# A fourth second-level product in a two-level Strassen MoE layer, with its mixtures, row transposes and output gates placed anew

## The chip, the cores and the metric

The kernel runs on one core of one Trainium2 chip. A core has five engines that work side by side, each through its own instructions in order: TensorE (PE) multiplies matrices and writes to PSUM, VectorE (DVE) and ScalarE (ACT) do elementwise work, GpSimd (POOL) issues the indirect DMAs here, and SyncE (SP) issues the plain ones. The metric is the device time of one execution in microseconds.

## The reference, cut to what matters

The input x is 8 sequences of 1024 tokens with 512 features, fp32. An attention layer with sine and cosine features comes first, and it is not touched here. Then follows a mixture of experts:

```python
x = x + attention(layernorm(x))
x = x + moe(layernorm(x))

# moe: 8 experts, 2 per token, at most 160 tokens of a sequence per expert
probs = softmax(x @ Wr + br); topk_p, topk_e = top_k(probs, 2)
buf = scatter(x)                          # (8 experts, 1280 rows, 512)
h = relu(einsum("enc,ech->enh", buf, W1) + b1)   # 512 -> 2048
y = einsum("enh,ehc->enc", h, W2) + b2           # 2048 -> 512
out = sum over a token's experts of topk_p * y
```

Each expert therefore multiplies 1280 rows by a 512 x 2048 and by a 2048 x 512 matrix, all in fp32.

## The kernel before, in words

Attention and most of the routing take the first 1260 us. The experts follow in 16 chunks, two per expert: a **long** chunk of 768 rows (`nh` = 3 blocks of 128 rows in each of two halves) and a **short** one of 512 rows (`nh` = 2). The even chunks 0, 2, ..., 14 are long, the odd ones short. `experts()` runs a chunk's first layer (`layer1`, eight steps `q`), and then its second layer.

Both layers use Strassen's scheme in Winograd's form: the two operands are cut into 2 x 2 blocks, and seven products p1 to p7 of sums and differences ("mixtures") of blocks take the place of eight. VectorE makes the mixtures: `mix_w1` for the first layer's weights, one step ahead; `mix_w2` for W2, in eight parts, for the expert to come, during a long chunk's first layer (one part in each step from the third on, the rest behind the eighth step); `gather` for the rows (the four row sums at L1185 to L1188). The hidden tile `hid` holds seven row parts (h11, h12, g4, h22, g1, g2, g3), which `p4` completes (relus on ScalarE at L1278 to L1281, sums on VectorE at L1282 to L1285).

In the second layer, `layer2` handles one block in each half with plain products (L1340); chunk 0 uses it for its three blocks, and each later long chunk for its third block. All other blocks go two at a time through `layer2_quad` (seven long chunks from chunk 2 on, and eight short ones). There a plain product is 32 matmuls of 256 columns (L1473). Three of the seven products, p2, p3 and p4, are cut once more by the same scheme: `mix` makes eight mixtures of 128 x 512 on VectorE (L1422 to L1429), and `second_level` runs seven chains of eight matmuls of 128 columns (L1439, through `chain`). In such a run three PSUM banks u, v and z are reused: a chain that adds onto u must wait until ScalarE has copied u out. ScalarE makes five copies (L1450, L1453, L1455, L1459, L1464), VectorE three adds (L1457, L1461, L1462). The counts of matmuls in the profile are two for each in the code, since an fp32 matmul shows as two.

The mixtures need room (`places`): a short chunk takes the unused columns of `hid`, a long one the rows' tiles `xe` and `xe_s`, which the first layer has finished with.

Rows arrive by an indirect DMA on GpSimd's queue (`fetch`), go through DRAM (`put_row`, `quarters` on SP's queue) and are transposed on VectorE (L1175). `gather` yields after each transpose; the generator `aside` carries it, and the second layer calls `next(aside)` between its products. A finished output row block is biased on VectorE, scaled by the router's probability on ScalarE (`gate`, L1310), and added to the output in DRAM by an indirect accumulating DMA on GpSimd's queue (`send`, L1315), two blocks in each half, first rows y1 and second rows y2.

The order on PE, ACT, DVE and SP is the order of the Python program (`manual_schedule`). GpSimd's instructions are placed by a planner. Pools are released tile by tile.

Of the kernel before, what the change touches and what calls it, by code (L numbers as in the profile page):

```python
# [73 lines left out]
def preln_attn_moe_kernel(  # L74
# [105 lines left out]
    load_x(0)  # L180
    ident = const.tile([P, P], F32, name="ident")
    make_identity(nc, ident)
# [1145 lines left out]

    def layer2(i, block, hid, aside):

        e = chunks[i][0]
        ws = w2_tiles[e]
        cols = slice(block * P, (block + 1) * P)

        def bank():
            return pools["ps_p"].tile([P, 512], F32, name="ps_p")[:, :DC]

        def product(ps, part, weight, first, last):
            for k in range(NHQ):
                nc.tensor.matmul(  # L1340
                    ps, lhsT=hid[:, k, part, cols], rhs=ws[weight][:, k, :],
                    start=first and k == 0, stop=last and k == NHQ - 1, skip_group_check=True,
                )
            next(aside, None)

        gate, send = outputs(i, block)
        (y1, y11, y12), (y2, y21, y22) = new_y(), new_y()
        low, high = b2_tiles[e][:, :DC], b2_tiles[e][:, DC:]

        def side_product():  # L1350
            side = bank()
            product(side, 1, 1, True, True)
            TT(y11, y11, side, ALU.add)

        plain_first = i == 0 and block == 0
        top = bank()
        product(top, 0, 0, True, False)
        nc.scalar.copy(y11, top)
        if plain_first:
            side_product()  # L1360
        mid = bank()
        product(mid, 4, 3, True, False)
        nc.scalar.copy(y22, mid)
        product(top, 5, 4, False, False)
        nc.scalar.copy(y12, top)
        if not plain_first:
            side_product()
            product(top, 6, 5, False, False)
            TT(y22, y22, top, ALU.add)
        product(mid, 2, 2, False, True)  # L1370
        TT(y12, y12, mid, ALU.add)
        TT(y1, y1, b2_tiles[e], ALU.add)
        gate(0, y1)
        send(0, y1)
        if plain_first:
            product(top, 6, 5, False, False)
            TT(y22, y22, top, ALU.add)
        TT(y22, y22, high, ALU.add)
        gate(1, y22)
        product(top, 3, 6, False, True)  # L1380
        TT(y21, top, low, ALU.add)
        gate(1, y21)
        send(1, y2)

    def places(i, hid):
# [15 lines left out]

    SECOND = [(1, 1), (2, 2), (3, 6)]

    def layer2_quad(i, hid, aside, before_last):

        e = chunks[i][0]
        ws = w2_tiles[e]
        free = places(i, hid)
        low, high = b2_tiles[e][:, :DC], b2_tiles[e][:, DC:]
        two = range(2)  # L1410

        def split(t, part_of):
            return [[part_of(t[:, 4 * k : 4 * k + 4], c) for c in two] for k in two]

        def mix(n):
            part, weight = SECOND[n]
            a = split(hid, lambda t, c: t[:, :, part, c * P : (c + 1) * P])
            b = split(ws[weight], lambda t, c: t[:, :, c * P : (c + 1) * P])
            (a11, a21), (a12, a22) = a
            (b11, b12), (b21, b22) = b  # L1420
            t1, t2, t3, t4, s2, s3, s4 = free[:7]
            TT(t1, b12, b11, ALU.subtract)  # L1422
            TT(s3, a11, a21, ALU.subtract)
            TT(a21, a21, a22, ALU.add)
            TT(t2, b22, t1, ALU.subtract)
            TT(s2, a21, a11, ALU.subtract)
            TT(t3, b22, b12, ALU.subtract)
            TT(s4, a12, s2, ALU.subtract)
            TT(t4, b21, t2, ALU.subtract)  # L1429
            return (  # L1430
                (a11, b11), (a12, b21), (s4, b22), (a22, t4), (a21, t1), (s2, t2), (s3, t3)
            )

        def bank():
            return pools["ps_p"].tile([P, 512], F32, name="ps_p")

        def chain(ps, pair, first):
            for k in range(4):
                nc.tensor.matmul(  # L1439
                    ps, lhsT=pair[0][:, k, :], rhs=pair[1][:, k, :], start=first and k == 0,  # L1440
                    stop=k == 3, skip_group_check=True,
                )

        def second_level(n, pairs):
            m1, m2, m3, m4, m5, m6, m7 = pairs
            c = free[7 + n]
            c11, c12, c21, c22 = (c[:, k, :] for k in range(4))
            u, v, z = (bank()[:, :P] for _ in range(3))
            chain(u, m1, True)
            nc.scalar.copy(c11, u)  # L1450
            next(aside, None) if n < 2 else None
            chain(v, m5, True)
            nc.scalar.copy(c21, v)  # L1453
            chain(u, m6, False)
            nc.scalar.copy(c12, u)  # L1455
            chain(z, m2, True)
            TT(c11, c11, z, ALU.add)  # L1457
            chain(u, m7, False)
            nc.scalar.copy(c22, u)  # L1459
            chain(v, m3, False)  # L1460
            TT(c22, c22, c21, ALU.add)  # L1461
            TT(c12, c12, v, ALU.add)  # L1462
            chain(u, m4, False)
            nc.scalar.copy(c21, u)  # L1464
            return [c[:, 2 * b : 2 * b + 2, :] for b in two]

        def as_pair(t):
            return t.rearrange("p (c n) -> p c n", n=P)

        def product(ps, part, weight, first, last):  # L1470
            for b in two:
                for k in range(NHQ):
# [5 lines left out]
                    )  # L1478

        gate, send = zip(*(outputs(i, b) for b in two))  # L1480
        some(2, aside)
        pairs = mix(0)
        top, mid = bank(), bank()
        of = lambda ps, b: ps[:, b * DC : (b + 1) * DC]
        y1, y11, y12 = zip(*(new_y() for _ in two))
        product(top, 0, 0, True, False)
        for b in two:
            nc.scalar.copy(y11[b], of(top, b))
        next(aside, None)
        product(mid, 4, 3, True, True)  # L1490
        some(3, aside)
        c = second_level(0, pairs)
        for b in two:
            TT(as_pair(y11[b]), as_pair(y11[b]), c[b], ALU.add)
        pairs = mix(1)
        product(top, 5, 4, False, False)
        for b in two:
            nc.scalar.copy(y12[b], of(top, b))
            TT(y12[b], y12[b], of(mid, b), ALU.add)
        c = second_level(1, pairs)  # L1500
        for b in two:
            TT(as_pair(y12[b]), as_pair(y12[b]), c[b], ALU.add)
        y2, y21, y22 = zip(*(new_y() for _ in two))
        for b in two:
            nc.scalar.copy(y22[b], of(mid, b))
        for b in two:
            TT(y1[b], y1[b], b2_tiles[e], ALU.add)
            gate[b](0, y1[b])
            send[b](0, y1[b])
        pairs = mix(2)  # L1510
        product(top, 6, 5, False, True)
        for b in two:
            TT(y22[b], y22[b], of(top, b), ALU.add)
            TT(y21[b], of(top, b), low, ALU.add)
            TT(y22[b], y22[b], high, ALU.add)
        before_last()
        c = second_level(2, pairs)
        for b in two:
            TT(as_pair(y21[b]), as_pair(y21[b]), c[b], ALU.add)
            gate[b](1, y22[b])  # L1520
            gate[b](1, y21[b])
            send[b](1, y2[b])


# [18 lines left out]
    def experts(ending):  # L1543
# [5 lines left out]
        for i, (e, j0, nh) in enumerate(chunks):  # L1549
            parts, box = box[0], [None]  # L1550
            hid = pools["hp"].tile([P, NHQ, 7, HALF], F32, name="hid")
            tiles = None
            ahead = rows_ahead(i + 1) if i and i + 1 < len(chunks) else iter(())
            for q in range(NHQ):
# [5 lines left out]
                if i and q > 1:  # L1560
                    next(mixes, None)
                next(ahead, None)
                tiles = layer1(Hidden(i, q, parts, hid, [ending]), tiles, q == NHQ - 1)
                if i == 0 and q == NHQ // 2:
                    rest(ending)
                    to_router.close()
                    for name, bufs in (("w2p", 1), ("yp", 4), ("bp", 1)):
                        pools[name] = to_end.pool(name, bufs, reuse_waits="tile", **left)
# [19 lines left out]
            if i:  # L1588
                layer2_quad(
                    i, hid, iter(()) if nh > 2 else aside, mix_next if nh == 2 else lambda: None  # L1590
                )
            for block in range(2 if i else 0, nh):
                if block == nh - 1:
                    mix_next()
                layer2(i, block, hid, aside)
            rest(aside)
# [253 lines left out]
```

## Time and profile before

| | |
|---|---|
| median of 3 runs | 3204.99 us (3201.2 to 3208.88) |
| the profiled execution | 3195.52 us; span 3193.8 us |
| PE busy | 3122.6 us (98%) |
| DVE busy | 2209.3 us (69%) |
| ACT busy | 1664.9 us (52%) |
| POOL busy | 426.8 us (13%) |
| a plain product in a quad, 32 matmuls | 6.91 us |
| a second-level run, 56 matmuls | 6.25 us |
| a long chunk: first layer, quad, third block | 72.25, 46.38, 24.18 us |
| a short chunk: first layer, quad | 48.35, 46.38 us |

How to read it: busy shares are averages over stages with different limits, so a share far below 100% says nothing of a stage. The chain that ended last is followed back from the last instruction, each step to what released it. In the profile's timelines a row gives start, length, engine, line, operation, output and inputs, and in brackets the idle time before it with what ended that. TensorE's matmuls are pipelined, so consecutive ones overlap in the timeline; the spacing of their starts is what they cost. A row with a count (x8) merges several instructions.

### The profile page before, as it was taken

Reading aid. Unit: us, or ns where it says so; the run is one execution under the profiler, and the core shown is the slowest. Engines: PE = TensorE matmul, PEld = TensorE weight load, DVE = VectorE, ACT = ScalarE, POOL = GpSimd, SP = SyncE. Lnnn points to the kernel's source line nnn. Section 1 sums busy time; section 2 is a strip of 40 time slices with the busy share of each in tenths; the row PEclk is TensorE's granted clock in tenths of the full one; section 3 lists DMA queues with packets and bytes.
Section 4 is the critical chain, followed back from the end, with each engine's and each line's share of the span. In section 5 each row is a group of like instructions: output and inputs, shape, how many; then the busy total and the mean of one; then the engine's idle time right before and its main releaser. Section 6 shows DMA issues by size and latency. Waiting matters only on the chain.

```text
span 3193.8 us, 51293 instructions
## 1 busy us (share of the span) xinstructions
PE 3122.6 (98%) x19726; PEld 2145.4 (67%) x19726; DVE 2209.3 (69%) x4643; ACT 1664.9 (52%) x2554; POOL 426.8 (13%) x387
## 2 busy tenths in 40 slices
PE   5999999999999999999999999999999999999998
PEld 2444444444444444689698698698698698698687
DVE  8888878888788775637657657656657656656654
ACT  7888888888888885413423423323323323323322
POOL 3000202020111123411011011011011011011010
PEclk9999999999999999999999999999999999999999
DMA  5435454554645353423423433434433334334331
GB/s 166 147 100 165 120 159 132 148 140 138 184 108 159 80 166 88 141 60 98 147 57 98 140 62 103 130 63 112 120 70 110 115 74 114 107 80 116 96 60 21
DMA packets 288547, 358.72 MB, mean 112 GB/s; under 512 B 28376, under 2 KB 199088, under 8 KB 276272
## 3 DMA queue, kind: packets, MB, share of 16 engines
q1 hardware_dynamic: 264944, 312.20, 33.3%
q0 software_dynamic: 22912, 43.22, 7.4%
q8 instruction: 157, 2.57, 0.4%
q14 instruction: 86, 0.70, 0.1%
q10 hardware_dynamic: 448, 0.02, 0.0%
HBM read 207.02 MB, written 81.22 MB: 90 GB/s over the span
## 4 chain that ended last, share of the span: by engine, by line
PE 79%; DVE 3%; ACT 1%; issue 1%; DMA 0%; SPq 0%; POOLq 0%; DVEq 0%; ACTq 0%
PE ps_p L1239 30%; PE ps_p L1473 13%; PE av L717 9%; PE ps_p L1439 9%; PE ps_s L683 9%; PE ps_p L1340 7%; ACT e L703 1%; PE ps_s L215 1%; PE ps_s L697 1%; DVE qk_f L524 1%; DVE qk_r L447 0%; DVE xT L837 0%; DMA qk<-qk_r 0%; DVE v L447 0%; SPq L608 0%
## 5 line engine op out<-in xcount | busy, mean ns | idle before, releaser
L703 ACT ACTIVATE e<-ps_s 128x1024 f32<-128x1024 f32 (+1 forms) x640 | 569.6, 937 | 183.3 <-PE ps_s L683 110.2
L683 PE MATMUL ps_s<-qk 64*128 64x512 f32 (+3 forms) x3072 | 597.3, 505 | 28.6 <-DMA qk<-qk_r 12.4
L717 PE MATMUL av<-e,v 128*64 128x512 f32 (+3 forms) x3072 | 523.4, 490 | 0.0
L683 PEld LDWEIGHTS ps_s<-qk 64*128 64x128 f32 x3072 | 262.3, 187 | 216.1 <-issue 106.4
L717 PEld LDWEIGHTS av<-e,v 128*64 128x64 f32 x3072 | 200.5, 137 | 283.1 <-issue 267.1
L1239 PE MATMUL ps_p<-xe,w 128*128 128x256 f32 (+1 forms) x1024 | 317.6, 433 | 1.1 <-issue 1.1
L1239 PE MATMUL ps_p<-xe_s,t 128*128 128x256 f32 (+1 forms) x1024 | 317.7, 433 | 0.0
L1239 PE MATMUL ps_p<-xe,t 128*128 128x256 f32 (+1 forms) x1024 | 317.7, 433 | 0.0
L1315 POOL DMA_INDIRECT out_dram<-y,slots x80 | 127.1, 1589 | 1234.0 <-ACT y L1310 1016.6
L768 POOL DMA_INDIRECT slot_d<-token,slot x128 | 159.2, 1244 | 988.5 <-issue 612.3
L1282 DVE TENSOR_TENSOR hid<-hid 128x256 f32<-128x256 f32 (+1 forms) x128 | 64.0, 500 | 283.0 <-ACT hid L1280 283.0
L1239 PEld LDWEIGHTS ps_p<-xe_s,t 128*128 128x128 f32 x1024 | 193.8, 190 | 82.0 <-ACT hid L1249 2.5
L1239 PEld LDWEIGHTS ps_p<-xe,t 128*128 128x128 f32 x1024 | 194.2, 190 | 80.4 <-issue 0.4
L1239 PEld LDWEIGHTS ps_p<-xe,w 128*128 128x128 f32 x1024 | 193.7, 190 | 79.4 <-issue 1.2
L1473 PE MATMUL ps_p<-w_t,hid 128*128 128x256 f32 x960 | 212.2, 379 | 0.0
L1473 PE MATMUL ps_p<-w,hid 128*128 128x256 f32 x960 | 209.6, 379 | 0.0
L1473 PEld LDWEIGHTS ps_p<-w,hid 128*128 128x128 f32 x960 | 182.4, 190 | 26.3
L1473 PEld LDWEIGHTS ps_p<-w_t,hid 128*128 128x128 f32 x960 | 180.1, 190 | 23.2
L1239 PE MATMUL ps_p<-xe_s,w 128*128 128x256 f32 (+1 forms) x512 | 158.9, 433 | 0.6 <-ACT p L1255 0.6
L1249 ACT COPY hid<-ps_p 128x256 f32<-128x256 f32 (+1 forms) x128 | 54.2, 423 | 179.6 <-PE ps_p L1239 170.9
L1340 PE MATMUL ps_p<-w,hid 128*128 128x256 f32 x640 | 144.8, 381 | 2.5 <-DVE w L1068 2.5
L697 PEld LDWEIGHTS <-keys_b 64*128 64x128 bf16 x1536 | 80.8, 95 | 89.5 <-issue 71.5
(300 smaller groups left out, 4959.6 us busy)
## 6 DMA issues: line engine op xcount, KB each, us to landing
w<-in_L_ffn_W_dram SPq DMA_DIRECT2D x256, 256.0 KB, 3.4
w<-in_L_ffn_W_dram SPq DMA_DIRECT2D x64, 512.0 KB, 7.4
qk<-qk_c SPq DMA_DIRECT2D x124, 256.0 KB, 4.5
qk<-qk_r SPq DMA_DIRECT2D x120, 256.0 KB, 4.5
qk_base<-base_d SPq DMA_DIRECT2D x28, 1024.0 KB, 7.5
xn_d<-xn SPq DMA_DIRECT2D x72, 256.0 KB, 2.4
rows_d<-xg SPq DMA_DIRECT2D x70, 256.0 KB, 2.1
x_mid<-in_L_attn_x_dram SPq DMA_DIRECT2D x16, 1024.0 KB, 8.9
```

The lines of the kernel that those rows point to most:

```text
L683: nc.tensor.matmul(ps[:, a, at : at + w], lhsT=pair[r, 1, kb * P : (kb + 1) * P], rhs=pair[r, 0, q0 : q0 + w], start=at == 0, stop=not own ...
L697: nc.tensor.matmul(out_, lhsT=keys_b[r, part, :], rhs=late, start=False, stop=part == 1, skip_group_check=True,)
L703: nc.scalar.activation(e, ps[:, :, :n], AF.Exp, scale=UNIT * UNIT / math.sqrt(2 * DH))
L717: nc.tensor.matmul(av[a * 64 : (a + 1) * 64, q0 - 512 * h :], lhsT=vt[:, kb, 2 * pr + a, :], rhs=es[i][:, a, at : at + w], start=kb == 0, ...
L768: queued = nc.gpsimd.indirect_dma_start(out=slot_d[b], out_offset=bass.IndirectOffsetOnAxis(ap=idx, axis=0), in_=src, in_offset=None,)
L1239: nc.tensor.matmul(ps, lhsT=weights[:, k, :], rhs=rows[:, k, :], start=first and k == 0, stop=last and k == 1, skip_group_check=True,)
L1249: nc.scalar.copy(self.blocks[0], self.top)
L1282: TT(g1, g3, h22, ALU.add)
L1315: ins = nc.gpsimd.indirect_dma_start(out=out, out_offset=bass.IndirectOffsetOnAxis(ap=meta[:, e, jj[r], 0:1], axis=0), in_=y, in_offset=No ...
L1340: nc.tensor.matmul(ps, lhsT=hid[:, k, part, cols], rhs=ws[weight][:, k, :], start=first and k == 0, stop=last and k == NHQ - 1, skip_group ...
L1439: nc.tensor.matmul(ps, lhsT=pair[0][:, k, :], rhs=pair[1][:, k, :], start=first and k == 0, stop=k == 3, skip_group_check=True,)
L1473: nc.tensor.matmul(ps[:, b * DC : (b + 1) * DC], lhsT=hid[:, k, part, b * P : (b + 1) * P], rhs=ws[weight][:, k, :], start=first and k == ...
```

## The change

The quad's fourth product, p5, is cut by the second level too. Its plain product, 32 matmuls of 256 columns, becomes a run of seven chains, 56 matmuls of 128 columns, and the bank `mid` that held it is gone; the result goes from a tile c5 into y12 and y22. The second level is now a class `Second` with `weights`, `left` (the eight mixtures), `both` (all eight in an interleaved order) and `run` (the seven chains), where `run` takes two callbacks: `between`, behind the first copy, and `late`, behind the fourth. In short chunks the weight mixtures of p5 and p2 are made during the first layer (`early_sums`), two in each of the steps 4 to 7; in long chunks p5's eight are made at the quad's start. The order of products in a quad is now p1, p5, p6, p2, p7, p3, p4; in long chunks two products of the third block stand ahead of p4, the others behind the quad.

W2's parts for the next expert are made one in each of the third and fourth steps of the long first layer, and two in each step from the fifth. The row transposes of a short chunk come two ahead of p5's run, one behind the next eight mixtures, one inside p2's run, one behind p4's mixtures, and the last one with the four row sums inside p3's run; in long chunks they come in two pairs among the third block's products. The gates of the right halves go behind the first copy of p4's run, and in short chunks the gates and sends of the first rows go behind its fourth copy. There are five y buffers in place of four, and the identity matrix moves to a pool that ends with the routing. `layer2` is a generator.

```diff
-    ident = const.tile([P, P], F32, name="ident")
+    ident = own.tile([P, P], F32, name="ident")
...
-    SECOND = [(1, 1), (2, 2), (3, 6)]
+    class Second:
+        OPERANDS = {2: (1, 1), 3: (2, 2), 4: (3, 6), 5: (4, 3)}
...
+        def weights(self):
...
+            for to, x1, x2 in ((t3, b22, b12), (t1, b12, b11), (t2, b22, t1), (t4, b21, t2)):
+                TT(to, x1, x2, ALU.subtract)
+                yield
+
+        def left(self):
...
+            for to, x1, x2, op in (
+                (s3, a11, a21, ALU.subtract), (a21, a21, a22, ALU.add),
+                (s2, a21, a11, ALU.subtract), (s4, a12, s2, ALU.subtract),
+            ):
+                TT(to, x1, x2, op)
+                yield
+
+        def both(self):
+            w, a = self.weights(), self.left()
+            for gen, count in ((w, 2), (a, 2), (w, 1), (a, 1), (w, 1), (a, 1)):
+                some(count, gen)
...
+        def run(self, c, between=lambda: None, late=lambda: None):
...
+            chain(u, a11, b11, True)
+            nc.scalar.copy(c11, u)
+            between()
+            chain(v, a21, t1, True)
+            nc.scalar.copy(c21, v)
+            chain(u, s2, t2, False)
+            nc.scalar.copy(c12, u)
+            chain(z, a12, b21, True)
+            TT(c11, c11, z, ALU.add)
+            chain(u, s3, t3, False)
+            nc.scalar.copy(c22, u)
+            late()
+            chain(v, s4, b22, False)
+            TT(c22, c22, c21, ALU.add)
+            TT(c12, c12, v, ALU.add)
+            chain(u, a22, t4, False)
+            nc.scalar.copy(c21, u)
...
-        some(2, aside)
-        pairs = mix(0)
-        top, mid = bank(), bank()
+        ask(2)
+        if last_part:
+            rest(second[5].left())
+        else:
+            rest(second[5].weights())
+            rest(second[5].left())
+        top = bank()
...
-        product(mid, 4, 3, True, True)
-        some(3, aside)
-        c = second_level(0, pairs)
+        if last_part:
+            rest(second[2].left())
+        ask(2)
+        five = second[5].run(c5)
+        second[3 if last_part else 2].both()
+        ask()
         product(top, 5, 4, False, False)
...
+        add_to(y12, five)
+        add_to(y11, second[2].run(c, ask))
+        second[4 if last_part else 3].both()
+        ask()
+        product(top, 6, 5, False, True)
...
+        add_to(y12, second[3].run(c, ask))
         for b in two:
             TT(y1[b], y1[b], b2_tiles[e], ALU.add)
...
+        if not last_part:
+            first_rows()
+            second[4].both()
+            some(2, extra)
+        before_last()
...
+        add_to(y21, second[4].run(c5, right_halves, first_rows if last_part else lambda: None))
         for b in two:
-            gate[b](1, y22[b])
             gate[b](1, y21[b])
             send[b](1, y2[b])
...
-                    next(mixes, None)
+                    some(1 if q < 4 else 2, mixes)
...
+                if 2 < q < 7:
+                    some(2, early_sums)
...
-                    for name, bufs in (("w2p", 1), ("yp", 4), ("bp", 1)):
+                    for name, bufs in (("w2p", 1), ("yp", 5), ("bp", 1)):
...
+                if nh > 2:
+                    some(2, aside)
+                    for step in range(5):
+                        if step == 4:
+                            mix_next()
+                        next(extra)
+                        if step < 2:
+                            some(2, aside)
```

Here `ask` advances `aside` in short chunks alone, `some(n, g)` takes n steps of a generator and `rest(g)` all that are left; `extra` is the third block's `layer2`; `right_halves` and `first_rows` are the gates, with the sends, named above; `before_last` makes the next chunk's first W1 mixtures in short chunks.

More of the change, by code (lines that the diff above doesn't have):

```diff
@@ L1 @@
+import itertools
 import math
@@ L1327, in new_y, with layer2 @@
         return y, y[:, :DC], y[:, DC:]
-    def layer2(i, block, hid, aside):
+    def layer2(i, block, hid):
         e = chunks[i][0]
@@ L1343, in product @@
                 )
-            next(aside, None)
         gate, send = outputs(i, block)
-        (y1, y11, y12), (y2, y21, y22) = new_y(), new_y()
+        y1, y11, y12 = new_y()
         low, high = b2_tiles[e][:, :DC], b2_tiles[e][:, DC:]
[L1350 to L1353, printed above, removed]
         plain_first = i == 0 and block == 0
@@ L1358, in layer2 @@
         nc.scalar.copy(y11, top)
+        yield
         if plain_first:
-            side_product()
+            side = bank()
+            product(side, 1, 1, True, True)
+            TT(y11, y11, side, ALU.add)
+            yield
         mid = bank()
         product(mid, 4, 3, True, False)
+        yield
+        y2, y21, y22 = new_y()
         nc.scalar.copy(y22, mid)
@@ L1365, in layer2 @@
         nc.scalar.copy(y12, top)
+        yield
         if not plain_first:
-            side_product()
+            side = bank()
+            product(side, 1, 1, True, True)
+            TT(y11, y11, side, ALU.add)
+            yield
             product(top, 6, 5, False, False)
             TT(y22, y22, top, ALU.add)
+            yield
         product(mid, 2, 2, False, True)
@@ L1374, in layer2 @@
         send(0, y1)
+        yield
         if plain_first:
@@ L1377, in layer2 @@
             TT(y22, y22, top, ALU.add)
+            yield
         TT(y22, y22, high, ALU.add)
@@ L1383, in layer2 @@
         send(1, y2)
+        yield
     def places(i, hid):
@@ L1400, in places, with split, __init__, chain @@
         ]
-    SECOND = [(1, 1), (2, 2), (3, 6)]
-    def layer2_quad(i, hid, aside, before_last):
-        e = chunks[i][0]
+    def split(t, part_of):
+        return [[part_of(t[:, 4 * k : 4 * k + 4], c) for c in range(2)] for k in range(2)]
+    class Second:
+        OPERANDS = {2: (1, 1), 3: (2, 2), 4: (3, 6), 5: (4, 3)}
+        def __init__(self, i, hid, which, w_room, a_room):
+            part, weight = self.OPERANDS[which]
+            self.a = split(hid, lambda t, c: t[:, :, part, c * P : (c + 1) * P])
+            self.b = split(
+                w2_tiles[chunks[i][0]][weight], lambda t, c: t[:, :, c * P : (c + 1) * P]
+            )
+            self.w_room, self.a_room = w_room, a_room
+        def weights(self):
+            (b11, b12), (b21, b22) = self.b
+            t3, t2, t4 = self.w_room[:3]
+            t1 = self.w_room[3] if len(self.w_room) > 3 else b12
+            self.t = t1, t2, t3, t4
+            for to, x1, x2 in ((t3, b22, b12), (t1, b12, b11), (t2, b22, t1), (t4, b21, t2)):
+                TT(to, x1, x2, ALU.subtract)
+                yield
+        def left(self):
+            (a11, a21), (a12, a22) = self.a
+            s2, s3, s4 = self.a_room
+            self.s = s2, s3, s4
+            for to, x1, x2, op in (
[3 more added lines that the diff above has]
+                TT(to, x1, x2, op)
+                yield
+        def both(self):
+            w, a = self.weights(), self.left()
+            for gen, count in ((w, 2), (a, 2), (w, 1), (a, 1), (w, 1), (a, 1)):
+                some(count, gen)
+            rest(w)
+            rest(a)
+            return self
+        def run(self, c, between=lambda: None, late=lambda: None):
+            (a11, a21), (a12, a22) = self.a
+            (b11, _), (b21, b22) = self.b
+            t1, t2, t3, t4 = self.t
+            s2, s3, s4 = self.s
+            c11, c12, c21, c22 = (c[:, k, :] for k in range(4))
+            def chain(ps, left, right, first):
+                for k in range(4):
+                    nc.tensor.matmul(
+                        ps, lhsT=left[:, k, :], rhs=right[:, k, :], start=first and k == 0,
+                        stop=k == 3, skip_group_check=True,
+                    )
+            u, v, z = (
+                pools["ps_p"].tile([P, 512], F32, name="ps_p")[:, :P] for _ in range(3)
+            )
+            chain(u, a11, b11, True)
[15 more added lines that the diff above has]
+            nc.scalar.copy(c21, u)
+            return [c[:, 2 * b : 2 * b + 2, :] for b in range(2)]
@@ new lines, in seconds, with layer2_quad @@
+    def seconds(i, hid):
+        free = places(i, hid)
+        if chunks[i][2] == 2:
+            rooms = [(free[6 * n : 6 * n + 3], free[6 * n + 3 : 6 * n + 6]) for n in range(2)]
+            results = free[12:14]
+        else:
+            rooms = [(free[:4], free[4:7])] * 2
+            results = free[7:9]
+        return {w: Second(i, hid, w, *rooms[n % 2]) for n, w in enumerate((5, 2, 3, 4))}, results
+    def layer2_quad(i, hid, second, aside, before_last):
+        e, _, nh = chunks[i]
@@ L1407, in layer2_quad @@
         ws = w2_tiles[e]
-        free = places(i, hid)
+        last_part = nh == 2
+        if second is None:
+            second = seconds(i, hid)
+        second, (c5, c) = second
         low, high = b2_tiles[e][:, :DC], b2_tiles[e][:, DC:]
         two = range(2)
[L1412 to L1432, printed above, removed]
@@ L1434, in bank @@
+        extra = layer2(i, 2, hid) if nh > 2 else iter(())
         def bank():
             return pools["ps_p"].tile([P, 512], F32, name="ps_p")
[L1437 to L1465, printed above, removed]
@@ L1467, in as_pair, with add_to @@
         def as_pair(t):
             return t.rearrange("p (c n) -> p c n", n=P)
+        def add_to(ys, parts):
+            for b in two:
+                TT(as_pair(ys[b]), as_pair(ys[b]), parts[b], ALU.add)
         def product(ps, part, weight, first, last):
@@ L1478, in product, with ask @@
                     )
+        def ask(count=1):
+            if last_part:
+                some(count, aside)
         gate, send = zip(*(outputs(i, b) for b in two))
-        some(2, aside)
-        pairs = mix(0)
-        top, mid = bank(), bank()
         of = lambda ps, b: ps[:, b * DC : (b + 1) * DC]
+        ask(2)
+        if last_part:
+            rest(second[5].left())
+        else:
+            rest(second[5].weights())
+            rest(second[5].left())
+        top = bank()
         y1, y11, y12 = zip(*(new_y() for _ in two))
@@ L1488, in layer2_quad @@
             nc.scalar.copy(y11[b], of(top, b))
-        next(aside, None)
-        product(mid, 4, 3, True, True)
-        some(3, aside)
-        c = second_level(0, pairs)
-        for b in two:
-            TT(as_pair(y11[b]), as_pair(y11[b]), c[b], ALU.add)
-        pairs = mix(1)
+        if last_part:
+            rest(second[2].left())
[3 more added lines that the diff above has]
+        ask()
         product(top, 5, 4, False, False)
@@ L1498, in layer2_quad, with first_rows, right_halves @@
             nc.scalar.copy(y12[b], of(top, b))
[L1499 to L1502, printed above, removed]
+        add_to(y12, five)
[3 more added lines that the diff above has]
+        product(top, 6, 5, False, True)
         y2, y21, y22 = zip(*(new_y() for _ in two))
         for b in two:
-            nc.scalar.copy(y22[b], of(mid, b))
+            TT(as_pair(y22[b]), as_pair(of(top, b)), five[b], ALU.add)
+            TT(y21[b], of(top, b), low, ALU.add)
+            TT(y22[b], y22[b], high, ALU.add)
+        add_to(y12, second[3].run(c, ask))
         for b in two:
             TT(y1[b], y1[b], b2_tiles[e], ALU.add)
[L1508 to L1511, printed above, removed]
-        for b in two:
[L1513 to L1519, printed above, removed]
-            gate[b](1, y22[b])
+        def first_rows():
+            for b in two:
+                gate[b](0, y1[b])
+                send[b](0, y1[b])
+        if not last_part:
[3 more added lines that the diff above has]
+        before_last()
+        def right_halves():
+            for b in two:
+                gate[b](1, y22[b])
+        add_to(y21, second[4].run(c5, right_halves, first_rows if last_part else lambda: None))
+        for b in two:
             gate[b](1, y21[b])
             send[b](1, y2[b])
+        return extra
     AHEAD = 2
@@ L1551, in experts @@
             hid = pools["hp"].tile([P, NHQ, 7, HALF], F32, name="hid")
-            tiles = None
+            tiles, second, early_sums = None, None, iter(())
+            if nh == 2:
+                second = seconds(i, hid)
+                early_sums = itertools.chain(second[0][5].weights(), second[0][2].weights())
             ahead = rows_ahead(i + 1) if i and i + 1 < len(chunks) else iter(())
@@ L1588, in experts @@
             if i:
-                layer2_quad(
-                    i, hid, iter(()) if nh > 2 else aside, mix_next if nh == 2 else lambda: None
-                )
[L1592 to L1595, printed above, removed]
+                extra = layer2_quad(
+                    i, hid, second, aside, mix_next if nh == 2 else lambda: None
+                )
+                if nh > 2:
[6 more added lines that the diff above has]
+                            some(2, aside)
+            else:
+                for block in range(nh):
+                    if block == nh - 1:
+                        mix_next()
+                    for _ in layer2(i, block, hid):
+                        next(aside, None)
             rest(aside)
```

## The prediction

> **What bounds the kernel now.** I read the page (busy shares, then the chain that ended last), then that chain in order of time, then the timelines of VectorE, ScalarE and GpSimd inside a second layer and at the end. Busy time, and the chain by engine:
>
> ```profile
> PE 3122.6 (98%) x19726; PEld 2145.4 (67%) x19726; DVE 2209.3 (69%) x4643; ACT 1664.9 (52%) x2554; POOL 426.8 (13%) x387
> ...
> PE 79%; DVE 3%; ACT 1%; issue 1%; DMA 0%; SPq 0%; POOLq 0%; DVEq 0%; ACTq 0%
> ```
>
> TensorE sets the end. The chain in order of time (start, length, what), for one short chunk's second layer and for the last one:
>
> ```profile
> 1945.18 13.81 PE ps_p L1473 x64
> 1958.99 6.25 PE ps_p L1439 x56
> 1965.24 6.91 PE ps_p L1473 x32
> 1972.15 6.25 PE ps_p L1439 x56
> ...
> 3166.08 6.91 PE ps_p L1473 x32
> 3172.99 6.26 PE ps_p L1439 x56
> 3180.62 4.77 DMA out_dram<-y,slots
> ```
>
> A plain product (L1473) takes 6.91, its second-level form (L1439) 6.25; TensorE never pauses. GpSimd's sends after the last product:
>
> ```profile
> 3168.48 1.60 POOL L1315 DMA_INDIRECT out_dram<-y,slots  x1 [76.89 <-ACT y L1310]
> 3174.05 1.56 POOL L1315 DMA_INDIRECT out_dram<-y,slots  x1 [3.98 <-issue]
> 3180.62 1.55 POOL L1315 DMA_INDIRECT out_dram<-y,slots  x1 [5.01 <-ACT y L1310]
> 3186.14 1.56 POOL L1315 DMA_INDIRECT out_dram<-y,slots  x1 [3.97 <-DMA out_dram<-y,slots]
> ```
>
> Each send waits until the one before has landed: 5.5 us apart at best. Two of the four lie under TensorE's work today. VectorE ahead of a long chunk's mixtures, and at the end of a short chunk's row work:
>
> ```profile
> 2067.19 0.56 DVE L1285 TENSOR_TENSOR hid<-hid 128x384 f32<-128x384 f32 x1
> ...
> 2071.69 0.69 DVE L1423 TENSOR_TENSOR xe<-hid 128x512 f32<-128x512 f32 x1
> 2072.41 0.69 DVE L1424 TENSOR_TENSOR hid<-hid 128x512 f32<-128x512 f32 x1
> ...
> 1973.26 1.11 DVE L1175 STREAM_TRANSPOSE xe<-xe_s 128x512 f32<-128x512 f32 x1
> ...
> 1978.26 0.28 DVE L1457 TENSOR_TENSOR hid<-hid,ps_p 128x128 f32<-128x128 f32 x1
> 1978.46 0.28 DVE L1461 TENSOR_TENSOR hid<-hid 128x128 f32<-128x128 f32 x1
> ```
>
> A mixture of 512 elements takes 0.69; the next starts 0.60 later, or 0.72 where it writes what its predecessor read (L1423, L1424) or reads what it wrote. One row transpose with the four row sums takes 5.00 (1973.26 to 1978.26).
>
> **What the Trainium skill says.** *TensorE: Matmul & The Clock Gate*, Step-by-step: the next weights load under the running matmul. It agrees: a chain's first weights load at 2078.24, its matmul at 2078.35. *VectorE: DVE Perf Modes*, The TRN2 errata: an fp32 tensor_tensor takes (N+151)/0.96 ns, 691 at 512; the trace has 684 to 692. *DMA: Bandwidth & Descriptors*, Rules for kernel authors: an accumulating DMA must wait for an earlier one on the same bytes, or an addition is lost. The waits above are that order.
>
> **The change part by part.** Seven long chunks (three token blocks a half) and eight short ones (two) have a quad. I count from the first matmul of the second layer (2063.64 in a long chunk, 1945.02 in a short one; the chain's starts are 0.17 later).
>
> *p5.* Fifteen products of 6.91 become 6.25: 15 x 0.66 = **-9.9**. New order in a short quad: p1 0 to 6.91, run of p5 to 13.16, p6 to 20.07, run of p2 to 26.32, p7 to 33.23, run of p3 to 39.48, run of p4 to 45.73; a long one has 6.91 of its third block ahead of the run of p4.
>
> *p5's mixtures, long chunk.* VectorE is free at 4.03 (2067.67; L1285 ends a chain that begins at TensorE's last first-layer product, so nothing earlier helps). Then come four weight mixtures, and s3, and only then a21, which the run's second chain loads. Intervals 0.60 + 0.72 + 0.72 + 0.60 + 0.72 = 3.36, so a21 starts at 7.39 and ends at 8.08; a waiting matmul starts 0.05 after VectorE's end (1352.10, 1352.16). The load is due at 6.91 + 0.78 = 7.69: 0.45 late, 7 x 0.45 = **+3.2** (bounds 0 and 4.5). s2 (8.80) is in time for the third chain. p1 covered these mixtures with 6.91; before, p1 and the plain p5 gave 13.81.
>
> *p5's mixtures, short chunk.* The eight weight mixtures of p5 and p2 run two a step in the first layer, steps 4 to 7: 1.2 us into 1.83 idle a step (L1282's wait for ScalarE). Nothing. The left sides end by 9, p5's run needs a21 at 7.6 and has it at 4.6.
>
> *W2 mixtures two per step*, long first layer: 1.71 more in a step of 9.03 with 2.17 idle. L1273 slips, and with it L1280 and L1282, by some 0.3 a step over three steps; banks turn over only after two steps, and step 8 has no mixtures left. The last weights are issued by 2009.5 and land in 8.8; they are wanted at 2028. Nothing.
>
> *Row transposes.* Short chunk: one transpose and the sums now sit inside the run of p3, behind which p4's run follows at once (in the kernel before, a 6.91 product followed them). VectorE: p2's last sum, 20.07 + 7.09 = 27.16; eight mixtures, 5.06, to 32.22; a transpose to 33.23; p7's six adds start 0.25 after 33.23 and take 2.0, to 35.48; transpose and sums to 40.48. Only then come the run's own adds, c22's at 40.68. ScalarE's last copy of that run waits for it (0.37 in the trace) to 41.05, so p4's first copy starts at 41.21 and ends at 41.48; its third chain, due at 39.48 + 1.78 = 41.26, may start at 41.53: 0.27 late. Seven chunks have rows to fetch: **+1.9** (bounds 0 and 5, as the list of some twenty intervals may be off by half a us). Long chunk: its pairs fall into the third block's remaining products; row loads are issued from 2110.98 on as now (eight of 0.43, landing in 2.5), by 7 after the quad, where the third transpose is wanted at 7.3. Nothing; a late load would be hidden for another 5 us.
>
> *ScalarE's gates.* The right halves' gates (0.42 each) go behind p4's first copy, and the copies behind them have a chain's slack: nothing. In short chunks the first rows' two gates and two sends move from ahead of the last run to behind its fourth copy. Within the program the four sends then end under the next first layer: the fourth starts some 16 after its start, and the next row fetch on GpSimd's queue is at 19.85 now (2011.41 after 1991.56), so nothing is pushed. SP's next bias load waits for the first rows' bias adds, at about 43 in the quad (42.9 now); the first-layer weights behind it keep a step's slack. In the last chunk there is no next layer to hide under. That copy starts 4.66 into the run (3177.49 after 3172.83), the gates at 4.82, the first send 1.00 later (3167.48, 3168.48): 5.82, or 0.43 before TensorE's end. Steps of 5.57, 5.55 and 5.5 put the fourth send 16.2 after it, and from a last send's start to the end it is 3193.8 - 3186.14 = 7.66: 23.9. Now it is 3193.8 - 3179.08 = 14.7. **+9.2** (bounds 8.5 and 10).
>
> *No cost:* a fifth y buffer, the identity's new pool, and chunk 0's generator (same products; its one pause, 0.51 at L1377's add, stays). VectorE gains some 85 us of work, ScalarE 10, hidden as listed.
>
> **Sum:** -9.9 + 3.2 + 1.9 + 9.2 = **+4.4** against the profiled execution's 3195.52 (span 3193.8). Its time is 9.5 below the median of the three runs, 3204.99; added to that, **3209.4**. About 0.2% (6.4 us) is what a measurement can tell from no change, and 4.4 lies below it.
>
> **Rivals.** *The saving stays (faster).* If the sends of different rows need not queue, or if y1's gates are passed early, the tail term vanishes; with stalls of 0 to 4 that leaves -10 to -6: 3195 to 3199. For it: 98% TensorE and an exact 0.66 a chunk. Against: the 3.97 wait on a send's DMA, and ScalarE's strict order.
>
> *VectorE takes over (slower).* Place: the run of p3 in short chunks, where TensorE goes on to p4 with no product between. Price: once ScalarE's copy is late, each us of VectorE's lateness is a us of TensorE's, seven times. My list has it 0.27 past the point already; from 0.6 late (2 us more in all) the whole is slower by over 0.2%. At 1.2 late: 4.4 + 7 x 0.93 = +10.9, 3216. For it: some 5.7 us more VectorE work in a quad of 45.73. Against: idle VectorE around p6 absorbs earlier delay.
>
> *The second level doesn't save.* If chains of 128 columns ran no faster for p5, 0 in place of -9.9: 3219. The three existing runs in all fifteen quads take 6.25, so this has hardly a chance.
>
> **How the numbers follow.** My case, within 0.2%: 0.52, its own range 3204 to 3211. Saving stays: 0.17. VectorE takes over: 0.29. Second level no faster: 0.02. The 8-in-10 range cuts both outer cases in part: 3198 to 3217. Faster 0.17, same 0.52, slower 0.31.
>
> **What the profile after would show.** The second-level line with 3360 matmuls and the plain one with 1440; TensorE's busy time some 10 lower; an idle of 0.3 to 0.5 before p5's second chain in long chunks alone, released by VectorE; an idle of 0.1 to 0.5 inside p4's run in short chunks with rows to fetch, released by ScalarE, and none in the last; four sends 5.5 apart, the first just before TensorE's end at some 3174, and 23 to 24 us behind it. I am wrong if two sends are done by then, if the pauses sum to over 8, or if TensorE pauses in a first layer.

## The result and the profile after

The changed kernel takes 3212.24 us (median of 22 runs, 3207.03 to 3214.41). The kernel before, run beside it, takes 3206.09 (22 runs), which is 1.1 more than its three runs shown above. The ratio is 1.0016, 95% interval 1.0009 to 1.0022: 5.1 us slower (2.9 to 7.1). That is below the 0.2% that I called no change, though the interval leaves out a ratio of 1.

The profiled execution took 3212.25 us, with a span of 3210.5, so it is an ordinary one; the one of before, 3195.52, was ten below its median. The two spans, 16.7 apart, therefore can't be compared as wholes. I split both at the first matmul of chunk 1 (as the chain counts it, 0.17 late in both) and at the end of TensorE's last matmul.

| us | before | after | difference |
|---|---|---|---|
| up to chunk 1 (code that the change hardly touches) | 1421.8 | 1433.5 | +11.7 |
| chunk 1 to TensorE's last matmul | 1757.5 | 1753.0 | -4.5 |
| from there to the end | 14.6 | 24.0 | +9.5 |

The first row is not the change's: a second profile of the changed kernel has 1421.6 there, and 1753.1 and 23.7 below it (see the experiments). The other two rows sum to +5.0, which is what the ratio shows; the two medians are 6.2 apart. Busy time after, and the chain by engine:

```profile
PE 3119.0 (97%) x20086; PEld 2150.0 (67%) x20086; DVE 2307.4 (72%) x4808; ACT 1681.0 (52%) x2599; POOL 425.8 (13%) x387
...
PE 76%; DVE 5%; ACT 2%; issue 1%; DMA 1%; SPq 0%; POOLq 0%; DVEq 0%; ACTq 0%
```

TensorE still sets the end, but VectorE and ScalarE now hold some of the chain. In order of time, TensorE's part of a short quad, the long chunk behind it, and the end:

```profile
1718.80 6.91 PE ps_p L1526 x32
...
1745.11 6.92 PE ps_p L1526 x32
1760.13 4.73 PE ps_p L1463 x40
1764.86 72.26 PE ps_p L1240 x224
1845.08 5.62 PE ps_p L1463 x48
...
3173.97 12.52 PE ps_p L1463 x112
3187.79 3.75 issue
3191.55 4.99 DMA out_dram<-y,slots
```

A plain product is L1526 now, and a second-level run is L1463. Two breaks are to be seen. Between 1752.03 and 1760.13 the chain leaves TensorE: it goes through VectorE and ScalarE, while TensorE works on and waits only at the end of that time. And of the first run of the long quad only 48 of its 56 matmuls are in TensorE's part, since the chain comes in through VectorE ahead of the second chain. In the last chunk, which has no rows to fetch, the two runs stand in one piece of 12.52.

GpSimd's sends at the end:

```profile
3185.89 1.55 POOL L1316 DMA_INDIRECT out_dram<-y,slots  x1 [87.47 <-ACT y L1311]
3191.55 1.56 POOL L1316 DMA_INDIRECT out_dram<-y,slots  x1 [4.10 <-issue]
3197.28 1.55 POOL L1316 DMA_INDIRECT out_dram<-y,slots  x1 [4.18 <-DMA out_dram<-y,slots]
3202.93 1.56 POOL L1316 DMA_INDIRECT out_dram<-y,slots  x1 [4.09 <-DMA out_dram<-y,slots]
```

TensorE's last matmul ends at 3186.5. All four sends now lie at or behind it, where two lay behind it before. For the third and fourth the profile names the landing of the send before as what ended the wait; for the second, at the same spacing, it names nothing.

### The profile page after: what moved, and what is told of

The parts are those of the page before. It is cut to its first block, busy times and chain, and to the rows that moved or that the text cites. A ratio compares the mean times of both kernels' runs of the same rounds, so it can differ in the third digit from the quotient of the medians.

```text
span 3210.5 us, 52221 instructions
## 1 busy us (share of the span) xinstructions
PE 3119.0 (97%) x20086; PEld 2150.0 (67%) x20086; DVE 2307.4 (72%) x4808; ACT 1681.0 (52%) x2599; POOL 425.8 (13%) x387
## 4 chain that ended last, share of the span: by engine, by line
PE 76%; DVE 5%; ACT 2%; issue 1%; DMA 1%; SPq 0%; POOLq 0%; DVEq 0%; ACTq 0%
PE ps_p L1240 30%; PE ps_p L1463 10%; PE av L718 9%; PE ps_s L684 9%; PE ps_p L1526 8%; PE ps_p L1341 7%; PE ps_s L216 1%; ACT e L704 1%; PE ps_s L698 1%; DVE qk_f L525 1%; DVE xe L1432 1%; DVE qk_r L448 0%; DMA out_dram<-y,slots 0%; DMA qk<-qk_r 0%; DVE xT L838 0%
## 5 line engine op out<-in xcount | busy, mean ns | idle before, releaser
L1526 PE MATMUL ps_p<-w_t,hid 128*128 128x256 f32 x960 | 212.2, 379 | 0.0
L1526 PEld LDWEIGHTS ps_p<-w_t,hid 128*128 128x128 f32 x960 | 180.1, 190 | 23.2
L1341 PE MATMUL ps_p<-w,hid 128*128 128x256 f32 x640 | 143.8, 380 | 3.0 <-DVE w L1069 3.0
L1463 PE MATMUL ps_p<-w,hid 128*128 128x128 f32 x1104 | 141.8, 275 | 0.0
L1463 PEld LDWEIGHTS ps_p<-w,hid 128*128 128x128 f32 x1104 | 135.9, 192 | 2.3
L1311 ACT ACTIVATE y<-y,slots 128x256 f32<-128x256 f32 (+1 forms) x120 | 66.1, 578 | 133.2 <-DVE y L1378 105.5
```

Source lines behind the costliest of these rows:

```text
L1311: nc.scalar.activation(part, part, AF.Identity, scale=meta[:, e, jj[r], 1:2].bitcast(F32))
L1341: nc.tensor.matmul(ps, lhsT=hid[:, k, part, cols], rhs=ws[weight][:, k, :], start=first and k == 0, stop=last and k == NHQ - 1, skip_group ...
L1463: nc.tensor.matmul(ps, lhsT=left[:, k, :], rhs=right[:, k, :], start=first and k == 0, stop=k == 3, skip_group_check=True,)
L1526: nc.tensor.matmul(ps[:, b * DC : (b + 1) * DC], lhsT=hid[:, k, part, b * P : (b + 1) * P], rhs=ws[weight][:, k, :], start=first and k == ...
```

## Experiments

All are edits of the changed kernel or of the kernel before. "Stretch" is the time from chunk 1's first matmul to TensorE's last one, and "tail" is what follows, both from each run's own profile. A ratio is to runs of the kernel before that were taken in the same session, which is one set of runs taken together. The interval of a ratio is too wide to tell the 2 or 3 us of a pause; the stretch can tell them, since in profiles of the same program it repeats to 0.1 us.

| run | stretch | tail | ratio to before, 95% |
|---|---|---|---|
| before (first profile) | 1757.5 | 14.6 | |
| before again, third, fourth time | 1757.5 each | 14.4, 14.5, 14.4 | |
| changed (first profile) | 1753.0 | 24.0 | 1.0016 (1.0009 to 1.0022) |
| changed again | 1753.1 | 23.7 | 1.0016 (1.0008 to 1.0024) |
| before, late first rows | 1757.5 | 23.5 | 1.0030 (1.0020 to 1.0040) |
| changed, early first rows | 1753.0 | 14.1 | 0.9986 (0.9978 to 0.9993) |
| changed, a21 early | 1749.9 | 23.7 | 1.0007 (0.9999 to 1.0016) |
| changed, sums early | 1750.8 | 24.1 | 1.0007 (0.9998 to 1.0015) |
| changed, a transpose twice | 1761.0 | 23.4 | 1.0037 (1.0025 to 1.0048) |
| changed, p5 plain | 1759.7 | 23.3 | 1.0032 (1.0021 to 1.0044) |
| all three edits | 1747.7 | 14.1 | 0.9968 (0.9955 to 0.9980) |
| all three again | 1747.7 | 13.9 | 0.9968 (0.9957 to 0.9980) |

**The two kernels again.** No edit.

> The changed kernel once more. Theory (the stated sum): from chunk 1's first matmul to TensorE's last one 1753 us, as in the first profile (1433.46 to 3186.50; before, 1757.5), and 24 us from there to the end. Before chunk 1 the first profile is 11.7 us later than the kernel before, with no instruction there changed in kind: 6 us in the attention and 5.6 in chunk 0, of which 4.5 is a pause of TensorE that nothing in the profile releases (1340.34). If these are chance, this execution shows another split, and no such pause; if the changed program causes them, the pause stands at the same matmul and chunk 1 begins near 1433 again.

> The kernel before once more, for its profile. If the attention's 6 us are chance, chunk 0 begins a few us away from the first profile's 1265; if not, within 1 us of it. The stretch from chunk 1 to TensorE's last matmul is 1757.5 us and the tail 14.6 in either case.

The changed kernel had chunk 1 at 1421.6 and no pause in chunk 0; the kernel before had chunk 0 at 1264.7, within 0.5 of the first time. The medians of that session were 3201.01 and 3195.58, both some 11 below the first ones, at the same ratio. So the 11.7 us ahead of chunk 1 are not fixed by the changed program.

**Late first rows in the kernel before.**

```diff
+        final = i + 1 == len(chunks)
+        if not final:
+            first_rows()
         pairs = mix(2)
...
-        c = second_level(2, pairs)
+        c = second_level(2, pairs, first_rows if final else lambda: None)
```

> The kernel before, with one edit: in the last chunk the first rows' gates and sends go behind the fourth copy of the last run. Theory (sends queue behind one another): the first send starts 0.4 to 0.6 us ahead of TensorE's last matmul, four sends 5.5 us apart follow, and the tail grows from 14.6 to 23.8 us: 9.2 us more in all. Rival (sends of different rows overlap, the tail is hidden): 0 us.

`first_rows` holds the gates and sends of y1, and `second_level` calls it behind c22's copy. The stretch stays and the tail grows by 8.9; the median goes from 3195.58 to 3205.05, 9.5 more. One edit at one place of the last chunk makes the kernel before 0.3% slower. Its sends:

```profile
3180.43 1.55 POOL L1315 DMA_INDIRECT out_dram<-y,slots  x1 [87.36 <-ACT y L1310]
...
3191.53 1.55 POOL L1315 DMA_INDIRECT out_dram<-y,slots  x1 [4.03 <-DMA out_dram<-y,slots]
```

**Early first rows in the changed kernel.**

```diff
         add_to(y11, second[2].run(c, ask))
...
+        final = i + 1 == len(chunks)
+        if final:
+            add_to(y12, second[3].run(c))
+            for b in two:
+                TT(y1[b], y1[b], b2_tiles[e], ALU.add)
+            first_rows()
         second[4 if last_part else 3].both()
         ask()
         product(top, 6, 5, False, True)
...
```

with p4's result in c in place of c5 for that chunk.

> The changed kernel, with one edit: in the last chunk p3's run goes ahead of p7, and the first rows' gates and sends follow it at once. Theory: two of the four sends lie under p7 and p4's run again, the tail is 14.6 us in place of 24.0, and TensorE's stretch from chunk 1 on stays at 1753: 9.4 us less than the changed kernel, some 4.4 less than the kernel before plus what chunk 0 and the attention add by chance. Rival (the tail's length is not from the late first rows): no change.

The tail is 14.1 again, and the stretch doesn't move. Two sends now start well ahead of TensorE's end, which is at 3173.8 here:

```profile
3163.01 1.60 POOL L1316 DMA_INDIRECT out_dram<-y,slots  x1 [77.32 <-ACT y L1311]
3168.69 1.56 POOL L1316 DMA_INDIRECT out_dram<-y,slots  x1 [4.08 <-issue]
```

The median is 3190.55 beside 3195.58 of before: 5.0 us faster. The late first rows are worth 9.6 to 9.9 in the tails, and to take them away is enough to turn the sign of the change.

**a21 early in long chunks.**

```diff
-            rest(second[5].weights())
-            rest(second[5].left())
+            second[5].both()
```

> The changed kernel, with one edit: at the start of a long chunk's quad p5's eight mixtures are made in the interleaved order that the other runs have (two weight mixtures, then two left ones), so that a21 is the fourth and not the sixth. Theory: a21 ends at about 6.6 us from the quad's start in place of 8.1, the weights load of the second chain is due at 7.7, and the pause of 0.43 us in each of seven long chunks goes: a long quad takes 45.73 in place of 46.16, 3.0 us less in all. Rival (the pause is from something else at the start of that run, such as ScalarE's copy of the first chain or a bank): 46.16 stays.

The stretch falls by 3.1 (3.0 expected): a long quad takes 45.73. In the changed kernel VectorE's order was this (two of each kind merged in a row):

```profile
1840.48 0.56 DVE L1286 TENSOR_TENSOR hid<-hid 128x384 f32<-128x384 f32 x1
1840.96 1.28 DVE L1432 TENSOR_TENSOR xe<-w 128x512 f32<-128x512 f32 x2
1842.28 1.42 DVE L1432 TENSOR_TENSOR xe<-w,xe 128x512 f32<-128x512 f32 x2
1843.61 0.69 DVE L1443 TENSOR_TENSOR xe<-hid 128x512 f32<-128x512 f32 x1
1844.33 0.69 DVE L1443 TENSOR_TENSOR hid<-hid 128x512 f32<-128x512 f32 x1
```

and TensorE's weights loads of the run:

```profile
1843.63 1.08 PEld L1463 LDWEIGHTS ps_p<-w,hid 128*128 128x128 f32 x8
1845.08 0.97 PEld L1463 LDWEIGHTS ps_p<-xe,hid 128*128 128x128 f32 x8 [0.37 <-DVE hid L1443]
```

The last VectorE row is a21; it ends at 1845.02, and the second chain's first load starts at 1845.08. a21 starts 3.85 behind L1286 there; with the edit it starts 2.40 behind it (1841.50 and 1839.10), the load has no wait, and the pause is gone:

```profile
1841.50 0.69 DVE L1443 TENSOR_TENSOR hid<-hid 128x512 f32<-128x512 f32 x1
1843.25 0.97 PEld L1463 LDWEIGHTS ps_p<-xe,hid 128*128 128x128 f32 x8
```

**Row sums early in short chunks.**

```diff
         second[3 if last_part else 2].both()
-        ask()
+        ask(2)
```

> The changed kernel, with one edit: one more row transpose of a short chunk goes behind the mixtures that follow p5's run, so that the last transpose and the row sums come ahead of p7's adds and not inside p3's run. Theory: c22's add of p3's run is no longer behind 5 us of row work, ScalarE's last copy comes in time, and the pause of 0.31 us in seven short chunks goes: a short quad takes 45.73 in place of 46.04, 2.2 us less in all. Rival (the pause is ScalarE's own, from the right halves' gates between the copies): 46.04 stays, since the gates are where they were.

The stretch falls by 2.2, as expected, and p3's and p4's runs stand in one piece of 12.50 in every short chunk, as here:

```profile
1752.61 12.50 PE ps_p L1463 x112
```

The gates between the copies stayed where they were, so they are not the cause.

**A row transpose twice.**

```diff
-                nc.vector.transpose(
+                for _ in range(2 if nh == 3 and j == 2 * nh - 1 else 1):
+                    nc.vector.transpose(
```

> The changed kernel, with the last row transpose of each long chunk's rows made twice (the same values again), 1.0 us more for VectorE inside p3's run in seven short chunks. Theory (VectorE's list is already past the point at which TensorE waits): each short quad grows by 1.0, from 46.04 to 47.05, 7 us more in all. Rival (some slack absorbs it, as it would wherever a plain product follows): less than 0.3 a quad.

The stretch grows by 8.0, 1.15 in each of seven chunks. The second transpose, on the target of the first, costs VectorE 1.14 and not 1.0 (from the transpose's start to the first row sum 2.29, from 1757.79 to 1760.08; in the changed kernel 1.15), so the slope is one to one. Its waits of TensorE:

```profile
PE ps_p L1464 <- ACT hid L1473: 8.4, 7, 1.2
...
PE ps_p L1464 <- DVE hid L1444: 1.3, 7, 0.2
```

The first is the wait for p4's first copy, seven times 1.2; the second is a21 in the long chunks. Such a wait is shorter than the pause that it stands for (1.2 for 1.47, 0.2 for 0.44): it is counted from the modelled end of the matmul before, 0.16 behind the moment at which the next one was due, and it leaves out 0.10 that TensorE loses at the restart (see below). There is no slack left at this place.

**p5 plain.**

```diff
-        five = second[5].run(c5)
+        mid = bank()
+        product(mid, 4, 3, True, True)
+        five = [c5[:, 2 * b : 2 * b + 2, :] for b in two]
+        for b in two:
+            nc.scalar.copy(five[b], as_pair(of(mid, b)))
```

without p5's mixtures in either kind of chunk.

> The changed kernel with p5 as a plain product again (32 matmuls of 256 columns, ScalarE copies it to c5; its eight mixtures are not made, nor is its run). Theory: p5 takes 6.91 in place of 6.25 in fifteen quads, 9.9 us more, and the pause of 0.43 in seven long chunks goes, 3.0 less, the one of 0.31 in short chunks stays: 6.9 us more than the changed kernel, TensorE's stretch from chunk 1 to its last matmul near 1760. Rival (p5's second level saves less than its matmuls say, since its mixtures slow other work): less than 4 us more, or none.

The stretch grows by 6.7: 9.9 for p5's products less 3.0 for the long chunks' pause is 6.9. p5's second level does save what its matmuls say. With p5 plain the stretch is still 2.2 longer than that of the kernel before: the pause in short chunks comes from the new order of the row work, not from p5's second level.

**All three edits.** Early first rows, a21 early and sums early together.

> The changed kernel with the three edits together (first rows early in the last chunk, a21 fourth in long chunks, row sums ahead of p7's adds in short ones). Theory: every quad takes 45.73, the tail is 14.6, and what is left of the change is 15 x 0.66 = 9.9 us: 0.31% less than the kernel before, ratio 0.997. Rival (something else in the change costs time): a ratio of 0.9985 or more.

> The changed kernel with the three edits once more, beside p5 plain. Theory: as before, ratio to the kernel before 0.997; chunk 0's pause stands or not with the chip, while the stretch from chunk 1 on is 1747.7 and the tail 14.6 in either case.

Both times the ratio is 0.9968, in a session where the kernel before takes 3208.62 (this one 3198.57) and in one where it takes 3195.88 (this one 3184.8). The stretch is 9.8 shorter than that of the kernel before, and the tail is 0.3 to 0.7 shorter. This version beats both kernels. Its short and long quads, in order of time:

```profile
1747.43 6.91 PE ps_p L1526 x32
1754.34 12.50 PE ps_p L1463 x112
1766.84 72.24 PE ps_p L1240 x224
1839.08 6.91 PE ps_p L1526 x32
1845.99 6.25 PE ps_p L1463 x56
```

**What stays open.**

> The kernel before a third time, for its profile. On the chip of the first profiles of before, chunk 0 starts near 1265 us and TensorE has no pause in chunk 0's first layer; in five profiles of the changed kernel and its variants the start is 5 to 6 us later and such a pause of 4 to 9 us stands there, and in two it doesn't, with the same program. Theory (this is the chip or the execution, not the change): on a chip whose runs of before are near 3206 us the kernel before shows both too. Rival (the change has it): the kernel before shows neither on such a chip. On a chip near 3195 us this run tells nothing.

> The kernel before a fourth time, for the same question as the third, which fell on a chip near 3195 us and told nothing. Theory: where runs of before are near 3206 us, chunk 0 starts near 1270 and TensorE pauses in chunk 0's first layer, in the kernel before as in the changed one. Rival: near 1265, and no such pause.

Both fell in sessions where the kernel before takes 3194 to 3197 us, so they tell nothing. Nor is "the chip" shown to be what differs: the sessions with 3208.62 and 3195.88 for the kernel before lie 16 minutes apart, and the record gives both the same chip number.

In five profiles (the first of the changed kernel, a21 early, sums early, a transpose twice, and the first of all three) chunk 0's first piece in the chain starts near 1270 and TensorE pauses for 4 to 7 us in chunk 0's first layer, beyond 1.3 us that it waits there in every profile; in the others neither is there, with the same programs (the changed kernel and all three edits were profiled both ways). In all five it is ScalarE that stands still first, for 6.2 to 10.6 us, ahead of its next copies (L1250, L1251 in a transpose twice, and in a21 early also L1273), and TensorE goes on 0.05 us after such a copy. The same copy in the changed kernel's first and second profile:

```profile
1344.30 0.48 ACT L1250 COPY hid<-ps_p 128x384 f32<-128x384 f32 x1 [8.28 <-remote]
1331.80 0.48 ACT L1250 COPY hid<-ps_p 128x384 f32<-128x384 f32 x1 [1.78 <-PE ps_p L1240]
```

"remote" is another core or a queue that the profile doesn't know. The medians say that the kernel before is as much slower in such a session, since the ratios are the same in both kinds. But no profile of the kernel before was taken in one, so what holds ScalarE there, and whether the kernel before has this pause, is not shown.

## Why the prediction was right

*The sign and size.* Forecast: no change, +4.4, 3209.4. Measured: +5.1 by the ratio, 5.0 by the stages. Of the 2.8 us between 3209.4 and 3212.24, 1.1 is the median of before, which rose with more runs, and 0.6 is the terms below; the rest is the 1.1 by which the two medians differ more than the stages do.

*p5, -9.9.* Right. The runs take 6.25, and p5 plain and all three edits give 9.7 (6.7 + 3.0) and 9.8.

*Long chunks, +3.2.* Right: a long quad (the second layer less 24.18 for its third block) takes 46.16 in place of 45.73, 7 x 0.43 = 3.0, and the order of the mixtures alone removes it.

*Short chunks, +1.9.* Right in mechanism, and 0.3 too small in all: 46.05 in place of 45.73, 7 x 0.32 = 2.2. My list put c22's add at 40.68 from the quad's first matmul; it came at 40.64 (1759.27, with the quad's first matmul at 1718.63, 0.17 ahead of the chain's 1718.80). ScalarE's copies followed as listed:

```profile
1756.52 0.27 ACT L1481 COPY hid<-ps_p 128x128 f32<-128x128 f32 x1 [1.52 <-PE ps_p L1463]
1759.64 0.27 ACT L1487 COPY hid<-ps_p 128x128 f32<-128x128 f32 x1 [2.85 <-DVE hid L1484]
1759.81 0.27 ACT L1472 COPY hid<-ps_p 128x128 f32<-128x128 f32 x1
```

The last row is p4's first copy, 41.18 in the quad where I had 41.21. TensorE's third chain went on 0.05 after its end, as a waiting matmul did in the kernel before:

```profile
1760.13 0.97 PEld L1463 LDWEIGHTS ps_p<-hid 128*128 128x128 f32 x8 [0.26 <-ACT hid L1472]
```

That is 41.50, where I had 41.53. So the list was, if anything, 0.03 too long; what it left out is the restart. The weights load and the matmul behind a wait start together in the record, and the second matmul starts 0.21 after the first, where all others of these runs follow at 0.11. This loss of 0.10 stands behind each of the fourteen waits. The long chunk's term has it, since there I counted from when the weights load was due; here I counted from when the matmul was due, so 0.23 became 0.33.

*The last chunk's sends, +9.2.* Right: 9.5 in the first two profiles, 9.4 in the second two. The first send starts 0.42 ahead of TensorE's end, counted as there (3185.42 + 0.89; 0.43 forecast), and the steps are 5.66, 5.73 and 5.65, some 0.1 to 0.2 us longer each than I had taken.

*What was costed at nothing.* The stretch is the sum of the costed terms (-9.8 + 3.1 + 2.3 = -4.4 from the stages unrounded, measured -4.5), so nothing is left for the first-layer mixtures, the long chunks' row pairs and the right halves' gates. From chunk 1 on, a first layer takes 48.35 or 72.24 in both kernels.

*The signs.* I had called myself wrong if TensorE paused in a first layer, and in the first profile it did, for 4.5 us in chunk 0. The second profile of the same program has no such pause, and no first layer from chunk 1 on has one in either, so the sign was set too wide. TensorE's busy time fell by 3.6 and not by some 10. From chunk 1 on it fell by 6.1, since of 5.4 us of pauses the profile shows only 1.6 as idle and counts the rest as busy; ahead of chunk 1 it rose by 2.5. VectorE's rose by 98, where I had 85.

*The rivals.* By the same sum, "the saving stays" would have come true with the two edits of the tail and of one pause (-9.8 and 2.3 or 3.1); that pair was not run. "VectorE takes over" named the right place, and the twice-made transpose shows its slope of one. The change stopped at 0.23 in that count, against the 0.6 from which that case began. That sends need not queue is ruled out for this program. Whether they must is not shown: the rule cited in the prediction is for the same bytes, and no run lets sends to different rows go unordered.

*What I had not foreseen* is the wide spread ahead of chunk 1 between sessions. No part of it shows in the ratio.

## What to carry to other kernels

When work leaves the bound engine, look at which products used to cover the other engines' lists: here one run followed another without a plain product between, and 0.33 us of the row work in that place was no longer covered; and the order of eight mixtures decided whether the one that TensorE needed first came in time. A group of transfers that wait for one another cost nothing in the middle of this program and 9.5 us at its end, so the last pass deserves an order of its own. A small saving repeated fifteen times (9.8 us) can be spent by one such end.

## What the runs showed of the hardware

Accumulating sends to the same output start 5.3 to 5.7 us apart when each waits for the one before, in every profile, and 7.3 to 7.7 us pass from the last one's start to the end of the span. A wait of TensorE inside a second-level run costs 0.10 us more than the wait: the second matmul behind it starts 0.21 after the first, in place of 0.11, in all fourteen cases of the changed kernel. VectorE's or ScalarE's end and TensorE's going on are 0.05 to 0.06 us apart (1845.02 and 1845.08, 1760.08 and 1760.13).

The same program differs by 13 us between sessions (3195.58 and 3208.62 for the kernel before), while the two ratios that were measured twice came out the same (1.0016 and 0.9968, each with an interval of some 0.001 to either side).
